# First attention of a four-layer kernel: plain products for the first keys, GpSimd's sums and loads in a written order, two roots on ScalarE, another order of the key and value products

## The chip, the cores and the metric

The kernel runs on one core of one Trainium2 chip. A core has five engines that work at the same time, each through its own instructions in order: TensorE (PE in the profile, with its weight loads as PEld), VectorE (DVE), ScalarE (ACT), GpSimd (POOL) and SyncE (SP), which here only starts transfers. The metric is the device time of one execution in microseconds (us). The time before is the median of three runs.

## The reference

Four layers work one after the other on `x` (2048 rows of 512 features, float32), each adding its result to `x`: cross attention, a feed-forward network, a second cross attention, a mixture of experts. The change is in the first:

```python
def _L0_xattn_ref(query, kv, Wq, bq, Wkv, bkv, Wo, bo):
    q = (query @ Wq + bq).reshape(B, L, NKV, G, HDIM)
    k_, v_ = jnp.split(kv @ Wkv + bkv, 2, axis=-1)
    ...
    scores = jnp.einsum('blkgd,bmkd->bkglm', q, k) * scale
    attn = jax.nn.softmax(scores, axis=-1)
    o = jnp.einsum('bkglm,bmkd->blkgd', attn, v).reshape(B, L, NHEAD * HDIM)
    return o @ Wo + bo

x = x + _L0_xattn_ref(_layernorm(x, axis=-1), ctx_4096, ...)
```

There are 32 sequences of 64 rows, 8 key/value heads (NKV) with 4 query heads each (G), and 128 features to a head.

## The kernel before, in words

The 2048 rows are four chunks of 512. The first attention goes through 32 steps `i`; a step is one chunk and one key/value head, and two chunks alternate: for chunks 0 and 1 the eight heads in turn, then the same for chunks 2 and 3. Step 16 is the first of chunk 2, step 17 the first of chunk 3.

**Products in seven parts.** A product of two matrices of 2 by 2 blocks needs eight block products. The kernel uses a scheme with seven, which needs sums and differences of blocks beforehand: `left_sums` makes three sums of the blocks of the left matrix and overwrites one block with a difference, `right_sums` does the same for the right one. Each is four operations. For the weights and the context they run on POOL, for the normalised rows and the attention output on DVE. The products are named after the blocks: "11", "12", "22" and "21" are blocks as they are, "1" to "4" are the sums.

**Where the operands come from.** `attn0_in(c)` prepares a chunk: statistics of the rows by `row_stats` (DVE, L363 and L364 for each of four tiles of 128 rows), the inverse square root of the variance by `inv_sqrt` (DVE: a first guess from the bits of the number, L346, then three rounds of three Newton operations, L353 to L355), the normalised rows `h_a` (DVE, L461), the addition of the output bias `bo` to `x` (POOL, L464), 16 transposes `pt_a` on PE (L468), four copies by ACT (L473), and the four sums on DVE (L424 to L427). `kv_left` makes the sums of a key or value weight for two heads, `ctx_right` those of a chunk of the context, `open_visit` those of the query weight, all on POOL; the output weight's sums follow (`visits[..]["o"]`).

**Making keys and values.** `attn0_kv` makes the keys (`value` 0) or the values (`value` 1) of two heads for one chunk, with seven products on PE (L520). Keys are 128 by 256 in a product, values two of 128 by 128. The products add up in PSUM banks `x`, `z` and two called `y` (`px`, `pz`, `py`, `pw` in the profile). `keep` copies a state of `x` to SBUF on ACT (`u_k`, `u_v`, L529 and L531), and `close` adds a bank and a kept state on DVE into one half of a head's tile (`kv`, L537). A bank that is added into again must first have been read. Of a key's matmuls of 128 by 256 the profile counts two passes each, so that a product is "x4".

**One step.** PE works through the queries of step `i` (`attn0_queries`: seven products of "x8" into `pqx`, `pqy`, `pqz`, `pqv`, L442; ACT adds the bias, L578; DVE closes into `qT_a`, L585), mixed with the turn of the last step's attention weights (`pt_o`, L639), their product with the values (`po_o`) and the output product (`attn0_out`: `ppx_o`, `ppy_o`, `ppz_o`; DVE adds to `x`, L672). After the queries come the scores (`sc_a`) and their softmax on DVE and ACT (L381 to L388). At the end of step `i`, `attn0_in` prepares the next step's chunk if it is new, and `make_kv` makes one set of keys or values. Before step 0 the kernel prepares chunk 0, the sums of the first key weight, the context of chunk 0, the first value weight, the query weight and the output weight, and makes the first keys.

**What sets the order.** A scheduler orders the instructions of each engine. An instruction that is wrapped in `pin` keeps the place that the program gives it among the other pinned ones of its engine. Before the change all of PE's products in this layer are pinned, but nothing on POOL, and on DVE none of the instructions named here. So the scheduler could take the statistics of chunks 2 and 3 early: they stand on DVE within the first 60 us.

**Loads.** SP starts the transfers in the order of the program: `x` of chunk 0, the first key weight, the context of chunk 0, the first value weight, the first query weight and output weight; `x` and context of chunk 1; `x` of chunks 2 and 3; then the weights of the next visit, and eight transfers of 4 MB that clear a buffer of the last layer (`xg<-zero`). A transfer waits until the eighth one before it has landed.

Of the kernel before, what the change touches and what calls it, by code (L numbers as in the profile page):

```python
# [16 lines left out]
P = 128  # L17
# [12 lines left out]
def layers(ctx: ExitStack, tc: tile.TileContext, a: dict, out: bass.AP):  # L30
# [81 lines left out]
    def rows(ap):  # L112
        return ap.rearrange("(k p) n -> p k n", p=P)

    def part(w, at, k, n):
        return w[:, at : at + k * n].rearrange("p (k n) -> p k n", k=k)

    def load_attn0(g, slot):
        w = weights[:, slot]
        wq, wo = part(w, 0, KT, 512), part(w, 3072, 4, HID)  # L120
        nc.sync.dma_start(wq, rows(a["Wq"][:, g * 512 : (g + 1) * 512]))
        nc.sync.dma_start(wo, rows(a["Wo"][g * 512 : (g + 1) * 512, :]))
        return wq, wo

    def load_kv(g, value):

        w = part(weights[:, value], 2048, KT, 2 * P)
        at = (value * NG + g) * P
        nc.sync.dma_start(w, rows(a["Wkv"][:, at : at + 2 * P]))
        return w  # L130
# [58 lines left out]
    def load_ctx(c, dst):  # L189
        src = rows(a["ctxT"][:, c * CH : (c + 1) * CH])  # L190
        if len(dst.shape) == 4:

            for j in range(2):
                for i in range(2):
                    nc.sync.dma_start(
                        dst[:, 2 * j + i], src[:, 2 * j : 2 * j + 2, i * 256 : (i + 1) * 256]
                    )
        else:
            nc.sync.dma_start(dst, src)

    for c in range(NC):
        for i in range(c * TT, (c + 1) * TT):
            nc.sync.dma_start(xs[i], a["x"][i * P : (i + 1) * P, :])
        if c == 0:
            w_k = load_kv(0, 0)
            load_ctx(0, ctx_q[0])
            w_v = load_kv(0, 1)
            w_next = load_attn0(0, 0)
        if c == 1:
            load_ctx(1, ctx_q[1])  # L210

    def constant(name, shape, src):
        t = const.tile(shape, F32, tag=name, name=name)
# [141 lines left out]
            nc.vector.scalar_tensor_tensor(y, u, 1.5, y, ALU.add, ALU.mult)  # L355
        return y

    def row_stats(tiles, name, rms=False):

        mv = small.tile([P, len(tiles), 2], F32, tag="mv", name=f"mv_{name}")  # L360
        for t, x in enumerate(tiles):
            st = small.tile([P, 6], F32, tag="bnst", name=f"st_{name}_{t}")
            nc.vector.bn_stats(st, x)  # L363
            nc.vector.bn_aggr(mv[:, t, :], st)  # L364
        v = small.tile([P, len(tiles)], F32, tag="var", name=f"v_{name}")
        if rms:


            nc.vector.tensor_scalar(
                v, mv[:, :, 1], 1.0 + EPS, EPS * EPS, ALU.mult, ALU.add  # L370
            )
        else:
            nc.vector.tensor_scalar(v, mv[:, :, 1], EPS, None, ALU.add)
        return mv, inv_sqrt(v, name)

    def softmax(dst, ps, scale, name):

# [9 lines left out]
        nc.vector.reciprocal(rs, sm)  # L387
        nc.vector.tensor_tensor(d3, d3, rs[:, :, None].broadcast_to([P, 8, 64]), ALU.mult)  # L388

    def chunk_stats(c, name, rms=False):  # L390
        return row_stats(xs[c * TT : (c + 1) * TT], name, rms)


    def q_heads(qT, h):
# [16 lines left out]
    def left_sums(engine, a11, a12, a21, a22, sums):  # L411

        s1, s2, s4 = sums if isinstance(sums, list) else (sums[:, i] for i in range(3))
        engine.tensor_tensor(s1, a21, a22, ALU.add)  # L414
        engine.tensor_tensor(s2, s1, a11, ALU.subtract)
        engine.tensor_tensor(a21, a11, a21, ALU.subtract)
        engine.tensor_tensor(s4, a12, s2, ALU.subtract)
        return {"11": a11, "12": a12, "22": a22, "1": s1, "2": s2, "3": a21, "4": s4}
# [31 lines left out]
    def w_quarters(w):  # L450

        return [w[:, 2 * i : 2 * i + 2, j * 256 : (j + 1) * 256] for i in range(2) for j in range(2)]

    def attn0_in(c):

        hx = rows_q[c % 2]
        mv, rstd = chunk_stats(c, f"a{c}")
        for t in range(TT):
            x = xs[c * TT + t]
            h = t2(f"h_a{c}_{t}")  # L460
            nc.vector.tensor_scalar(  # L461
                h, x, mv[:, t, 0:1], rstd[:, t : t + 1], ALU.subtract, ALU.mult
            )
            nc.gpsimd.tensor_tensor(x, x, bo, ALU.add)  # L464
            pt = ps_mm(f"pt_a{c}_{t}")
            for k in range(KT):
                pin(
                    nc.tensor.transpose(  # L468
                        pt[:, k * P : (k + 1) * P], h[:, k * P : (k + 1) * P], ident
                    )  # L470
                )

            nc.scalar.copy(  # L473
                hx[:, t // 2 : t // 2 + 3 : 2, :, (t % 2) * P : (t % 2) * P + P],
                pt.rearrange("p (i k n) -> p i k n", i=2, k=2),
            )
        return right_sums(nc.vector, hx[:, 0], hx[:, 1], hx[:, 2], hx[:, 3], hx[:, 4:7])
# [16 lines left out]
    def kv_left(w, value):  # L494

        k11, k12, k21, k22 = (
            w[:, 2 * j : 2 * j + 2, i * P : (i + 1) * P] for i in range(2) for j in range(2)
        )
        return left_sums(nc.gpsimd, k11, k12, k21, k22, kv_sums[value])

    def ctx_right(c):
        x = ctx_q[c % 2]
        return right_sums(nc.gpsimd, x[:, 0], x[:, 1], x[:, 2], x[:, 3], ctx_sums[c % 2])

    def attn0_kv(value, g, c, left, right):
        n = f"{'kv'[value]}{g}_{c}"
        for i in range(2):
            kv[value, g + i, c] = kv_free.pop(0)
        dst = [kv_tiles[:, kv[value, g + i, c], :] for i in range(2)]

        def product(ps, x, y, first=True):
            x, y = left[x], right[y]
            for m in range(2 if value else 1):
                for k in range(2):
                    sides = (y[:, k, m * P : (m + 1) * P], x[:, k, :]) if value else (
                        x[:, k, :], y[:, k, :]
                    )
                    out_ps = ps[:, m * P : (m + 1) * P] if value else ps[:, 0:256]
                    pin(
                        nc.tensor.matmul(  # L520
                            out_ps, *sides, start=first and m == k == 0, stop=k == 1,
                            skip_group_check=True,
                        )
                    )

        def keep(ps, i, name):
            u = t2(f"{name}_{n}")[:, 0:256]
            if value:
                nc.scalar.copy(u, ps[:, 0:256])  # L529
            else:  # L530
                nc.scalar.activation(  # L531
                    u, ps[:, 0:256], AF.Identity, bias=bkv[:, g + i : g + i + 1]
                )
            return u

        def close(i, half, ps, u):
            nc.vector.tensor_tensor(  # L537
                dst[i][:, half * 256 : half * 256 + 256], ps[:, 0:256], u, ALU.add
            )

        x = ps_tr(f"px_{n}")
        product(x, "11", "11")
        u1 = keep(x, 0, "u1")
        y = ps_mm(f"py_{n}")
        product(y, "12", "21")
        close(0, 0, y, u1)
        product(x, "2", "2", first=False)
        u2 = keep(x, 0, "u2")
        z = ps_mm(f"pz_{n}")
        product(z, "1", "1")  # L550
        product(x, "3", "3", first=False)
        u3 = keep(x, 1, "u3")
        close(1, 1, z, u3)
        y = ps_mm(f"pw_{n}")
        product(y, "22", "4")
        close(1, 0, y, u3)
        product(z, "4", "22", first=False)
        close(0, 1, z, u2)

    def kv_use(value, g, c):  # L560

# [4 lines left out]
    def attn0_queries(g, c, left, right):  # L566
# [15 lines left out]
            return u  # L582

        def close(heads, half, ps, u):
            nc.vector.tensor_tensor(  # L585
                q5[:, heads, :, 4 * half : 4 * half + 4, :],
                ps.rearrange("p (m b q) -> p m b q", m=2, q=64),
                u.rearrange("p (m b q) -> p m b q", m=2, q=64),
                ALU.add,
            )  # L590

        x = ps_tr(f"pqx_{n}")
# [111 lines left out]
    def open_visit(v):  # L704

        w = w_next
        k11, k12, k21, k22 = w_quarters(w[0])
        visits[v] = {"w": w, "q": left_sums(nc.gpsimd, k11, k21, k12, k22, wq_sums)}

    def kv_chunk(p, j):  # L710

# [4 lines left out]
        attn0_kv(value, g, c, kv_lefts[value], ctx_rights[c])  # L716

    rights = {0: attn0_in(0)}
    kv_lefts = [kv_left(w_k, 0), None]
    ctx_rights = {0: ctx_right(0)}  # L720
    kv_lefts[1] = kv_left(w_v, 1)
    open_visit(0)
    visits[0]["o"] = right_sums(nc.gpsimd, *w_quarters(visits[0]["w"][1]), wo_sums)
    make_kv(0, 0, 0)
    last = None
    NP = NC // 2 * NG // 2
    for i in range(len(order) + 1):
# [46 lines left out]
        if i + 1 < len(order):  # L774
            cn, gn = order[i + 1]
            if cn not in rights:
                rights[cn] = attn0_in(cn)

        p, step = divmod(i, 4)
        if i == 0:  # L780
            ctx_rights[1] = ctx_right(1)
            make_kv(0, 0, 1)
        if step < 2:
            make_kv(1, p, step)
# [884 lines left out]
```

## Time and profile before

| | us |
|---|---|
| time, median of 3 runs | 1995.72 (1993.96 to 1996.13) |
| the profiled execution | 1996.16 |
| its span, first to last instruction | 1994.5 |
| PE busy | 1894.7 |
| DVE busy | 1060.4 |
| POOL busy | 545.8 |
| ACT busy | 506.0 |
| mean granted clock of PE | 0.983 |

The span's 40 slices of 50 us each (a digit is the busy share in tenths, in the row PEclk the clock that PE was granted):

```profile
PE   4999999999999999999999999999999999979993
PEclk8999999999999999999999999999999999989997
```

The first attention takes slices 1 to 25, and the first slice stands out. The rest of the span is the three other layers, which the diff does not touch. A line of a timeline gives start, duration, engine, line, operation, what is written and read, and how many; in brackets how long the engine was idle before and who ended it. A line of the waits gives the waiting engine, line and tile, who ended the wait, the sum, the number and the longest.

### The profile page before, as it was taken

The page shows a single profiled execution, that of the slowest core. Times are in us where ns is not written, and L with a number is a line of the kernel's source. Part 1 is how long each engine was busy: PE and PEld are TensorE (multiplying, and loading weights), DVE is VectorE, ACT ScalarE, POOL GpSimd, SP SyncE. Part 2 cuts the span into 40 slices and gives each one's busy share as a digit, 9 for nine tenths or more (in the row PEclk, how much of TensorE's full clock was granted, in tenths as well). Part 3 has the DMA queues.
Part 4 walks back from the last instruction along what each step waited for, and adds up shares of the span by engine and source line. Part 5 has one row for each costly group of instructions (what it writes and reads, how often), then busy time and mean ns, then how long its engine had stood idle before and what let it go on. Part 6 is the DMA issues. An engine that isn't in the chain of part 4 may idle for free.

```text
span 1994.5 us, 26636 instructions
## 1 busy us (share of the span) xinstructions
PE 1894.7 (95%) x10556; PEld 1544.1 (77%) x10556; DVE 1060.4 (53%) x2095; ACT 506.0 (25%) x985; POOL 545.8 (27%) x581
## 2 busy tenths in 40 slices
PE   4999999999999999999999999999999999979993
PEld 3888988988988888888888898687778777645441
DVE  7554454454456654454454456555466466773415
ACT  1222122122112212112112121311221565542221
POOL 8211211211322311211211212141444535540115
PEclk8999999999999999999999999999999999989997
DMA  9696111111211111100110012100004201224628
GB/s 322 191 306 189 43 32 32 43 32 32 64 53 33 43 32 32 43 33 32 43 32 22 22 52 63 50 1 12 1 22 137 64 12 54 70 85 132 216 92 272
DMA packets 129882, 151.72 MB, mean 76 GB/s; under 512 B 4704, under 2 KB 84384, under 8 KB 129760
## 3 DMA queue, kind: packets, MB, share of 16 engines
q1 hardware_dynamic: 118752, 122.70, 19.5%
q0 software_dynamic: 5392, 17.11, 2.6%
q10 hardware_dynamic: 5616, 10.23, 1.4%
q8 instruction: 84, 1.38, 0.3%
q14 instruction: 38, 0.31, 0.0%
HBM read 92.60 MB, written 56.36 MB: 75 GB/s over the span
## 4 chain that ended last, share of the span: by engine, by line
PE 87%; DVE 6%; ACT 2%; DMA 2%; issue 1%; POOL 1%; POOLq 0%; ACTq 0%; DVEq 0%
PE ppx_o L442 11%; PE pqx_a L442 8%; PE py L106 6%; PE sc_a L106 6%; PE pqz_a L442 6%; PE ppz_o L442 6%; PE po_o L106 3%; PE pp L106 3%; PE ppy_o L442 3%; PE pdx_f L442 3%; PE pqv_a L442 3%; PE pqy_a L442 3%; PE px_v L520 2%; PE phx_f L442 2%; PE px_k L520 2%; PE pz_v L520 2%
## 5 line engine op out<-in xcount | busy, mean ns | idle before, releaser
L383 ACT ACTIVATE at_a<-at_a 128x512 f32<-128x512 f32 x64 | 40.3, 631 | 442.5 <-DVE at_a L382 442.5
L106 PE MATMUL py<-arena,xT 128*128 x312 | 140.8, 593 | 0.6 <-DVE y L1404 0.4
L442 PE MATMUL pqz_a<-arena 128*128 128x256 f32 x512 | 122.8, 383 | 8.9 <-DVE qT_a L585 8.9
L442 PE MATMUL ppx_o<-weights,oT_o 128*128 128x256 f32 x512 | 122.8, 383 | 0.1
L578 ACT ACTIVATE u_a<-pqx_a,bq 128x256 f32<-128x256 f32 x192 | 80.6, 471 | 165.6 <-PE pqx_a L442 83.1
L106 PEld LDWEIGHTS sc_a<-kv,qT_a 128*128 128x128 f32 x1024 | 120.4, 193 | 1.8
L442 PE MATMUL pqx_a<-arena,weights 128*128 128x256 f32 x512 | 121.0, 379 | 0.0
L106 PE MATMUL sc_a<-kv,qT_a 128*128 128x64 f32 x1024 | 118.7, 274 | 0.0
L442 PEld LDWEIGHTS pqz_a<-arena 128*128 128x128 f32 x512 | 98.3, 192 | 22.8 <-issue 9.3
L672 DVE TENSOR_TENSOR x<-ppx_o,x 128x512 f32<-128x512 f32 x128 | 86.9, 679 | 43.3 <-PE ppx_o L442 38.5
L442 PEld LDWEIGHTS ppx_o<-weights,oT_o 128*128 128x128 f32 x512 | 94.8, 190 | 12.0 <-ACT oT_o L662 0.5
L585 DVE TENSOR_TENSOR qT_a<-pqz_a,u_a 128x512 f32<-128x512 f32 x64 | 44.2, 691 | 112.4 <-ACT u_a L578 79.2
L442 PEld LDWEIGHTS pqx_a<-arena,weights 128*128 128x128 f32 x512 | 94.9, 190 | 11.6
L106 PEld LDWEIGHTS py<-arena,xT 128*128 128x128 f32 x312 | 56.1, 190 | 56.7 <-issue 56.2
L424 POOL TENSOR_TENSOR arena<-weights 128x512 f32<-128x512 f32 x16 | 20.3, 1271 | 273.0 <-PE ppz_o L442 273.0
L585 DVE TENSOR_TENSOR qT_a<-pqy_a,u_a 128x512 f32<-128x512 f32 x32 | 22.1, 691 | 121.4 <-PE pqy_a L442 121.4
L414 POOL TENSOR_TENSOR arena<-weights 128x512 f32<-128x512 f32 x18 | 22.9, 1273 | 218.0 <-PE pqz_a L442 213.7
L414 POOL TENSOR_TENSOR kv_room<-weights 128x256 f32<-128x256 f32 x16 | 12.1, 758 | 254.8 <-DMA weights<-in_Wkv 254.7
L1404 DVE TENSOR_TENSOR y<-py,weights 128x512 f32<-128x512 f32 x39 | 26.9, 691 | 84.9 <-PE py L106 77.2
L381 DVE TENSOR_REDUCE mx_a<-sc_a 128x8 f32<-128x512 f32 x64 | 44.3, 692 | 45.1 <-PE sc_a L106 45.1
L106 PE MATMUL po_o<-atT_o,kv 64*128 64x256 f32 x512 | 65.9, 392 | 0.8 <-ACT atT_o L641 0.8
L953 POOL TENSOR_TENSOR s_f<-s_f,arena 128x512 f32<-128x512 f32 x16 | 21.4, 1359 | 157.0 <-DVE s_f L950 117.1
(402 smaller groups left out, 4242.8 us busy)
## 6 DMA issues: line engine op xcount, KB each, us to landing
xg<-zero SPq DMA_DIRECT2D x8, 4096.0 KB, 20.7
weights<-in_Wq SPq DMA_DIRECT2D x16, 1024.0 KB, 5.3
weights<-in_Wo SPq DMA_DIRECT2D x16, 1024.0 KB, 5.3
xr<-xg SPq DMA_DIRECT2D x39, 256.0 KB, 3.2
yg<-y ACTq DMA_DIRECT2D x39, 256.0 KB, 2.8
weights<-in_Wkv SPq DMA_DIRECT2D x16, 512.0 KB, 3.5
arena<-in_W_e SPq DMA_DIRECT2D x8, 1024.0 KB, 6.6
x<-in_x SPq DMA_DIRECT2D x16, 256.0 KB, 5.6
```

Source lines behind the costliest of these rows:

```text
L106: nc.tensor.matmul(ps, lhsT, rhs, start=(i == 0), stop=(i == len(pairs) - 1))
L381: nc.vector.tensor_reduce(mx, p3, AX.X, ALU.max)
L383: nc.scalar.activation(dst, dst, AF.Exp, scale=scale)
L414: engine.tensor_tensor(s1, a21, a22, ALU.add)
L424: engine.tensor_tensor(t1, b12, b11, ALU.subtract)
L442: nc.tensor.matmul(ps[:, m, :], left[:, k, m * P : (m + 1) * P], right[:, k, :], start=first and m == i == k == 0, stop=i == len(pairs) - ...
L520: nc.tensor.matmul(out_ps, *sides, start=first and m == k == 0, stop=k == 1, skip_group_check=True,)
L578: nc.scalar.activation(u[:, m * 256 : (m + 1) * 256], ps[:, m * 256 : (m + 1) * 256], AF.Identity, bias=bq[:, 4 * g + 2 * heads + m : 4 * ...
L585: nc.vector.tensor_tensor(q5[:, heads, :, 4 * half : 4 * half + 4, :], ps.rearrange("p (m b q) -> p m b q", m=2, q=64), u.rearrange("p (m ...
L672: nc.vector.tensor_tensor(dst, ps.rearrange("p (m n) -> p m n", m=2), dst, ALU.add)
L953: nc.gpsimd.tensor_tensor(y, y, gamma, ALU.mult)
L1404: pin(nc.vector.tensor_tensor(y, py, be1[:, bass.ds(v[1], 1), :], ALU.add))
```

## The change

- **First keys.** `make_kv(0, 0, 0)` is replaced by `attn0_first_keys`: for each of the two heads one plain product over all 512 features, 128 by 512, and one eviction by ACT with the bias. It needs no sums.
- **POOL's order.** In the start all of POOL's sums and bias adds are pinned, through the class `InOrder`, in this order: query weight, first key weight, context of chunk 1, first value weight, context of chunk 0, bias of chunk 0, output weight, and after step 0's scores the bias of chunk 1. After that POOL is free again. The bias adds leave `attn0_in` and become `add_bias`.
- **Loads.** The first query weight stands before the first value weight, and the latter and the first output weight are moved behind `x` and the context of chunk 1.
- **Roots.** For chunks 0 and 1 `first_inv_sqrt` takes a logarithm and an exponential on ACT and one round of Newton on DVE. Chunks 2 and 3 keep `inv_sqrt`.
- **Statistics.** For chunks 2 and 3 the statistics are pinned, and so is DVE's `close` of the queries, everywhere.
- **Key and value products.** `z`'s first product and its own kept state come right after `x`'s first; `z` gets its second product after `x`'s second, and the last one is `x`'s third. There are four kept states instead of three, in two tiles instead of three. `close` uses other pairs of bank and kept state.

```diff
         if c == 0:
             w_k = load_kv(0, 0)
             load_ctx(0, ctx_q[0])
-            w_v = load_kv(0, 1)
-            w_next = load_attn0(0, 0)
+            w_next = load_queries0(0, 0)
         if c == 1:
             load_ctx(1, ctx_q[1])
+            w_v = load_kv(0, 1)
+            w_next = w_next, load_out0(0, 0)
...
+    def first_inv_sqrt(v, name):
+
+        y = small.tile(v.shape, F32, tag="rsqrt", name=f"rs_{name}")
+        nc.scalar.activation(y, v, AF.Ln)
+        nc.scalar.activation(y, y, AF.Exp, scale=-0.5)
...
+        nc.vector.tensor_tensor(u, y, y, ALU.mult)
+        nc.vector.tensor_tensor(u, u, half, ALU.mult)
+        nc.vector.scalar_tensor_tensor(y, u, 1.5, y, ALU.add, ALU.mult)
+        return y
...
-            nc.vector.bn_stats(st, x)
+            stats = nc.vector.bn_stats(st, x)
+            if pinned:
+                pin(stats)
...
+    class InOrder:
+
+
+        def tensor_tensor(self, *operands):
+            pin(nc.gpsimd.tensor_tensor(*operands))
+
+    adder = [InOrder()]
+
+    def add_bias(c):
+        for x in xs[c * TT : (c + 1) * TT]:
+            adder[0].tensor_tensor(x, x, bo, ALU.add)
...
-        mv, rstd = chunk_stats(c, f"a{c}")
+        roots = first_inv_sqrt, inv_sqrt
+        mv, rstd = chunk_stats(c, f"a{c}", root=roots[c // 2], pinned=c > 1)
...
-            nc.gpsimd.tensor_tensor(x, x, bo, ALU.add)
...
         x = ps_tr(f"px_{n}")
         product(x, "11", "11")
-        u1 = keep(x, 0, "u1")
+        u1 = keep(x, 0, 0)
+        z = ps_mm(f"pz_{n}")
+        product(z, "1", "1")
+        z1 = keep(z, 1, 1)
         y = ps_mm(f"py_{n}")
         product(y, "12", "21")
         close(0, 0, y, u1)
         product(x, "2", "2", first=False)
-        u2 = keep(x, 0, "u2")
-        z = ps_mm(f"pz_{n}")
-        product(z, "1", "1")
-        product(x, "3", "3", first=False)
-        u3 = keep(x, 1, "u3")
-        close(1, 1, z, u3)
+        u2 = keep(x, 0, 2)
+        product(z, "4", "22", first=False)
+        close(0, 1, z, u2)
         y = ps_mm(f"pw_{n}")
         product(y, "22", "4")
+        product(x, "3", "3", first=False)
+        u3 = keep(x, 1, 3)
+        close(1, 1, x, z1)
         close(1, 0, y, u3)
-        product(z, "4", "22", first=False)
-        close(0, 1, z, u2)
+
+    def attn0_first_keys(g, c, w):
+
+        x = ctx_q[c % 2]
+        for i in range(2):
+            kv[0, g + i, c] = kv_free.pop(0)
+            ps = ps_mm(f"pk_{g + i}_{c}")
+            accumulate_next(
+                ps.rearrange("p (i n) -> p i n", i=2),
+                [
+                    (w[:, k, i * P : (i + 1) * P], x[:, k // 2 * 2 : k // 2 * 2 + 2, k % 2, :])
+                    for k in range(KT)
+                ],
+            )
+            nc.scalar.activation(
+                kv_tiles[:, kv[0, g + i, c], :], ps, AF.Identity,
+                bias=bkv[:, g + i : g + i + 1],
+            )
...
-            nc.vector.tensor_tensor(
-                q5[:, heads, :, 4 * half : 4 * half + 4, :],
...
+            pin(
+                nc.vector.tensor_tensor(
+                    q5[:, heads, :, 4 * half : 4 * half + 4, :],
...
     rights = {0: attn0_in(0)}
+    attn0_first_keys(0, 0, w_k)
+    open_visit(0)
     kv_lefts = [kv_left(w_k, 0), None]
-    ctx_rights = {0: ctx_right(0)}
+    ctx_rights = {1: ctx_right(1)}
     kv_lefts[1] = kv_left(w_v, 1)
-    open_visit(0)
-    visits[0]["o"] = right_sums(nc.gpsimd, *w_quarters(visits[0]["w"][1]), wo_sums)
-    make_kv(0, 0, 0)
+    ctx_rights[0] = ctx_right(0)
+    add_bias(0)
+    visits[0]["o"] = right_sums(adder[0], *w_quarters(visits[0]["w"][1]), wo_sums)
...
                 rights[cn] = attn0_in(cn)
+                if cn > 1:
+                    add_bias(cn)
...
         if i == 0:
-            ctx_rights[1] = ctx_right(1)
+            add_bias(1)
+            adder[0] = nc.gpsimd
             make_kv(0, 0, 1)
```

The diff leaves the loads of later visits and the three other layers as they are.

## The prediction

> **What bounds the kernel now.** I read the page, then the waits by engine, then the timeline of the first 110 us, of two steady rounds and of the place where chunks 2 and 3 enter.
>
> ```profile
> PE 1894.7 (95%) x10556; PEld 1544.1 (77%) x10556; DVE 1060.4 (53%) x2095; ACT 506.0 (25%) x985; POOL 545.8 (27%) x581
> ```
>
> TensorE (PE) is the bound. From 100 to 1200 us it is busy more than 99.4 us in every 100, so time can come only from PE's gaps. The waits of PE that lie in the code of the diff:
>
> ```profile
> PE pqz_a L442 <- DVE qT_a L585: 8.9, 1, 8.9
> PE px_k L520 <- POOL kv_room L425: 6.8, 1, 6.8
> PE pz_k L520 <- DVE kv L537: 3.8, 16, 0.6
> ```
>
> The first two are single gaps of the start, the third a small one met in each key product. In the timeline (start, duration):
>
> ```profile
> 11.24 2.89 PE L468 MATMUL pt_a<-ident,h_a 128*128 128x128 f32 x12 [11.24 <-DVE h_a L461]
> 15.84 1.45 DVE L424 TENSOR_TENSOR arena<-arena 128x512 f32<-128x512 f32 x1 [1.39 <-ACT arena L473]
> 17.83 1.71 POOL L424 TENSOR_TENSOR kv_room<-arena 128x512 f32<-128x512 f32 x1
> 23.75 2.08 PE L520 MATMUL px_k<-kv_room 128*128 128x256 f32 x4 [6.84 <-POOL kv_room L425]
> 50.27 3.75 PE L442 MATMUL pqz_a<-arena 128*128 128x256 f32 x8 [8.90 <-DVE qT_a L585]
> ```
>
> The gap before 23.75 waits for GpSimd's (POOL) sums, which stand behind its bias adds. The one before 50.27 waits for VectorE (DVE), which had the statistics of chunks 1, 2 and 3 and their roots in front of `qT_a`. DVE and POOL slow each other: a DVE sum of two SBUF tiles takes about 0.69 us alone and 1.45 here, POOL's 1.27 becomes 1.71. The PE timeline goes on:
>
> ```profile
> 74.37 1.04 PE L639 MATMUL pt_o<-ident,at_a 128*128 128x128 f32 x8
> ...
> 146.02 1.05 PE L520 MATMUL px_k<-arena,weights 128*128 128x256 f32 x4
> 146.91 1.03 PE L520 MATMUL pw_k<-kv_room,weights 128*128 128x256 f32 x4
> 148.16 1.13 PE L520 MATMUL pz_k<-arena,kv_room 128*128 128x256 f32 x4 [0.22 <-DVE kv L537]
> 149.13 1.04 PE L639 MATMUL pt_o<-ident,at_a 128*128 128x128 f32 x8
> ```
>
> 74.37, the first `pt_o`, ends the start. Products of four key matmuls begin 0.86 us apart, the last only after 1.25: it adds into `z`, which DVE must first have read. Where chunk 2 enters:
>
> ```profile
> 628.43 0.68 DVE L388 TENSOR_TENSOR at_a<-at_a,rs_a 128x512 f32<-128x512 f32 x1
> 628.49 1.91 PE L468 MATMUL pt_a<-ident,h_a 128*128 128x128 f32 x16
> 629.03 0.68 DVE L672 TENSOR_TENSOR x<-ppx_o,x 128x512 f32<-128x512 f32 x1
> ```
>
> PE transposes at 628.49 without waiting: `h_a` was made from 607.59 to 618.15, from statistics taken at 44 to 48 us. DVE adds the last product of the round only after that. And what a gap costs beyond itself (stretch, length, PE, PEld, DVE, ACT, POOL, granted clock, DMA, GB/s):
>
> ```profile
> 44.00:48.00 4.00, 0.00 (x0) 0.00 (x0) 3.86 (x14) 0.00 (x0) 0.00 (x0) 0.67 1.15 346
> 48.00:52.00 4.00, 1.73 (x4) 1.49 (x5) 4.00 (x10) 0.00 (x0) 2.73 (x2) 0.50 0.25 75
> 52.00:56.00 4.00, 4.00 (x18) 3.55 (x17) 2.96 (x9) 0.00 (x0) 1.84 (x2) 0.55 0.00 0
> 56.00:60.00 4.00, 4.00 (x39) 4.00 (x38) 2.31 (x5) 1.15 (x3) 0.69 (x1) 1.00 0.00 0
> ```
>
> The clock falls to 0.5 some 4 us into the gap and is back at about 55.6, 5.3 us after work resumed: half of that, 2.7, is lost. After the gap of 6.84 us the same reckoning gives 2.3. I take 2.5.
>
> **The change, part by part.**
>
> *Start.* I follow the new order on each engine. Loads: the first transfers land at 256 KB per 0.69 us in the order issued (`x` 4 to 7 at 22.2 to 24, chunk 1's context at 25.0 to 27.2). So with the second Wkv and Wo moved behind chunk 1, Wq (1 MB, 2.75 us) lands behind the first context (14.6) at 17.4 instead of 18.8, `x` 4 to 7 from 18.0 to 20.1, context 1 from 20.8 to 22.9, Wkv at 24.3, Wo at 27.0. The later SP items keep their places and total.
>
> Root: six of nine Newton steps (0.2 us each) and the bit trick leave DVE, two ScalarE (ACT) operations come. No such small one is in the trace; a 128x256 one from SBUF takes 0.415, a 128x512 one 0.631, so 128x4 is about 0.2 by the line through them (bounds 0 and 0.415). With a hand-over each way the root is 0.7 us shorter (0.2 to 1.1). POOL's bias adds are gone from beside `h_a`, so four of them take 4 x 0.52 rather than 3.83: PE's transposes end at 12.5, ACT's four copies at 14.0, DVE's four sums at 16.6 (POOL idles until Wq).
>
> First keys: two products of K=512, 16 passes of 128x512 at 0.43 us (rows `py` of the experts: eight begin in 3.43) are 6.9 us, against 6.05 for seven shared ones, but need none of POOL's sums. They start when context 0 is there, 13.2, and end at 20.1. Queries: seven products of 1.73 us from 20.1. POOL's Wq sums (17.5 + 4 x 1.27 = 22.6) come in time. ACT now holds `pk_1`'s eviction and the first `u_a` behind the root of chunk 1, which waits for `x` 7 and DVE to 21.5: PE loses 0.2. DVE has three Newton steps, two contended `h_a` (1.42 each) and the closes; the last query product waits for one of them 0.1, the scores 0.9. Scores 32.6 to 37.0, transposes to 38.7 (before: 60.1), keys of chunk 1 38.7 to 45.3.
>
> Now DVE is late: softmax, its multiplication and the four sums of chunk 1, six operations with two SBUF tiles against POOL's row of sums and bias adds, 1.4 to 1.7 each, put the close that frees `py_v`'s bank at 51.0, where PE wants it at 47.0: 4 us. `pt_o` begins at 55.6. **Start: 74.4 - 55.6 = -18.8.** Bounds: -23 without that wait; -13.5 with the half clock after it (2.5) and Wq landing behind `x` 4 to 7 (2.75). POOL's remaining list (context 0, bias 0, Wo sums, bias 1; 16 x 1.27 and what DVE takes) ends near 61; Wo's sums are wanted by the third product of `attn0_out`, near 74. If that cover were gone, PE would wait one for one.
>
> *Order of the key and value products.* `z`'s second product now comes three products after its eviction, and the last closes fall under `pt_o`. A key bank takes 6.56 us now (142.57 to 149.13) against 7 x 0.865 = 6.05, a value bank 6.60 against 6.25. In the steady part are 14 and 15 of them: **-12.4** (7.1 + 5.3). The fourth eviction (0.37 to 0.47 on ACT, 25% busy) and `u3` after the last product lie under `pt_o` and two query products. Bound: 0, if `pt_o` has to wait instead.
>
> *Statistics of chunks 2 and 3.* They are pinned, and so are DVE's closes, so DVE can't take them early: the built order has them behind the round's last add. PE's transposes stand next. Chunk 2: with T the start of the last product, the add begins at T+1.93, the first statistics at T+2.65; three more at 0.79; from the last statistics to `h_a` 3.26 (rows 7.29 to 10.55, the root stays on DVE), to the transposes 0.69 (10.55 to 11.24): T+8.97 instead of T+1.73. Wait 7.2 and clock 2.5: **+9.7**. Chunk 3: seven statistics of the next stage and their small operations stand between; back to back at 0.6 and 0.1 to 0.2, `h_a` starts 9.6 after the first: T+12.94, wait 11.2, clock 2.5: **+13.7**. Upper bound there: eleven at 0.79 and thirty small at 0.21 are 15.0, wait 16.6. Lower: 9. The cover lost is 20 us of DVE's spare time.
>
> Row: after 50.27 real products ran, at half clock for 5.3 us. [...] The sum takes 2.5.
>
> *Bias adds* of chunks 2 and 3 go behind their transposes on POOL (27% busy), under the next 20 us of PE.
>
> **Sum**: -18.8 - 12.4 + 9.7 + 13.7 = **-7.8**. The profiled run took 1996.16 (span 1994.5 and 1.66 around it), 0.44 over the median; from the median, 1995.72 - 7.8 = **1988**.
>
> **Rivals.**
> 1. *The bank waits only move* (slower). Place: the end of each key or value set, `pt_o` waiting for closes. Price 12.4: 1995.7 - 18.8 + 23.4 = 2000; it decides from 7.8 kept, 0.27 per bank. For it: three evictions and three closes still end behind the last product. Against: `pt_o`'s two banks were read products earlier. 0.12.
> 2. *The start gives less*: -13.5, so 1993. For it: ACT and DVE work in order behind chunk 1's root. Against: landings follow the order of issue. 0.18.
> 3. *No wait at `py_v`*: -23, 1984. For it: in the steady part DVE's contended sums took 1.1 to 1.2. 0.15.
> 4. [...] 0.10.
>
> **How the numbers follow.** The forecast has 0.45, its own range 1983 to 1993. A measurement here tells 0.2% (4 us) from no change: faster is under 1991.7, slower over 1999.7. Faster: 0.42 of the forecast, all of rival 3, a third of rival 2: 0.63. Slower: most of rival 1 and some of 4: 0.13. Between: 0.24. Range 1980 to 1998: rivals 2, 3 and 4 are in it, rival 1's upper end is not.
>
> **What would show it.** The first `pt_o` near 55.6, no long PE wait before 38, one of some 4 us at `py_v`; key banks of 6.05 and value banks of 6.25; PE waits of 7 and 11 us at `pt_a` behind `h_a` for chunks 2 and 3, with the clock at 0.5 after each. I am wrong if those two waits are missing (then 1965) or `pt_o` comes after 62.

## The result, and the profile after

The changed kernel takes 1987.36 us (median of nine runs, 1986.13 to 1991.57). The kernel before took 1996.13 us beside it (1993.96 to 2005.25). The ratio is 0.9947 with a 95% interval of 0.9929 to 0.9964, so the kernel is faster by 0.4 to 0.7%: 8.8 us between the medians, some 11 by the ratio. The prediction said 1988 and faster. The profiled execution took 1988.88 us, its span is 1987.0.

Small as it is, this is the sum of two large amounts. Page of the changed kernel, busy time of each engine, and from its waits by engine two lines (sum, number of times, longest):

```profile
PE 1888.4 (95%) x10544; PEld 1545.4 (78%) x10544; DVE 1056.9 (53%) x2077; ACT 519.9 (26%) x1019; POOL 548.3 (28%) x581
```

```profile
PE pt_a L502 <- DVE h_a L496: 28.2, 5, 10.3
...
PE py_v L554 <- DVE kv L573: 3.6, 1, 3.6
```

The waits at `pqz_a`, `px_k` and `pz_k` that the page of before led with are gone. `pt_a` now leads: its 28.2 us hold the 10.3 us up to the first `h_a` of all (11.2 before) and two new waits for chunks 2 and 3. The timeline of TensorE (PE), changed kernel, shows the start and one steady key bank (start, duration):

```profile
10.34 3.65 PE L502 MATMUL pt_a<-ident,h_a 128*128 128x128 f32 x16 [10.34 <-DVE h_a L496]
13.78 7.49 PE L106 MATMUL pk<-arena,weights 128*128 128x512 f32 x16
21.11 1.89 PE L464 MATMUL pqx_a<-arena,weights 128*128 128x256 f32 x8
...
33.45 3.84 PE L106 MATMUL sc_a<-kv,qT_a 128*128 128x64 f32 x32
...
38.88 1.03 PE L554 MATMUL px_k<-arena,weights 128*128 128x256 f32 x4
...
50.45 1.16 PE L554 MATMUL py_v<-weights,arena 128*128 128x128 f32 x8 [3.57 <-DVE kv L573]
...
55.01 1.04 PE L696 MATMUL pt_o<-ident,at_a 128*128 128x128 f32 x8
...
122.87 1.03 PE L554 MATMUL px_k<-arena,weights 128*128 128x256 f32 x4
...
128.91 1.04 PE L696 MATMUL pt_o<-ident,at_a 128*128 128x128 f32 x8
```

The start ends at 55.01 instead of 74.37, the two gaps of 6.84 and 8.90 us in it are gone, and one of 3.57 at `py_v` has come. A key bank takes 128.91 - 122.87 = 6.04 us instead of 6.56. What was paid for it stands where chunk 2 enters. First VectorE (DVE), then PE, changed kernel:

```profile
603.29 0.69 DVE L729 TENSOR_TENSOR x<-ppx_o,x 128x512 f32<-128x512 f32 x1
603.90 0.68 DVE L383 BATCH_NORM_STATS2 st_a<-x 128x6 f32<-128x512 f32 x1
...
609.40 3.82 DVE L496 TENSOR_SCALAR h_a<-x,mv_a,rs_a 128x512 f32<-128x512 f32 x4
```

```profile
601.36 1.89 PE L464 MATMUL ppx_o<-arena,oT_o 128*128 128x256 f32 x8
610.09 2.95 PE L502 MATMUL pt_a<-ident,h_a 128*128 128x128 f32 x12 [6.83 <-DVE h_a L496]
613.37 1.08 PE L502 MATMUL pt_a<-ident,h_a 128*128 128x128 f32 x4 [0.33 <-DVE h_a L496]
614.25 1.62 PE L554 MATMUL px_k<-arena,weights 128*128 128x256 f32 x4
...
662.20 2.95 PE L502 MATMUL pt_a<-ident,h_a 128*128 128x128 f32 x12 [10.35 <-DVE h_a L496]
```

DVE begins the statistics only after the round's last addition to `x`; before, `h_a` was ready long ahead. PE stands for 6.83 us, in chunk 3 for 10.35, and goes on slowly: 16 transposes take 4.16 us (610.09 to 614.25) instead of 1.75. The clock tells why. Stretches of the changed kernel around both waits (stretch, length, PE, PEld, DVE, ACT, POOL, granted clock, DMA, GB/s):

```profile
604.00:608.00 4.00, 0.00 (x0) 0.00 (x0) 3.74 (x13) 0.00 (x0) 0.00 (x0) 1.00 0.00 0
608.00:612.00 4.00, 1.91 (x9) 1.64 (x10) 3.74 (x11) 0.59 (x1) 1.98 (x2) 0.58 0.00 0
612.00:616.00 4.00, 3.67 (x15) 3.01 (x15) 2.11 (x2) 1.80 (x4) 3.57 (x3) 0.57 0.00 0
616.00:620.00 4.00, 4.00 (x20) 3.53 (x19) 2.77 (x6) 1.38 (x3) 0.00 (x0) 1.00 0.00 0
...
654.00:658.00 4.00, 0.00 (x0) 0.00 (x0) 3.96 (x15) 0.00 (x0) 0.00 (x0) 0.80 0.16 61
658.00:662.00 4.00, 0.00 (x0) 0.00 (x0) 4.00 (x26) 0.00 (x0) 0.00 (x0) 0.50 0.00 0
662.00:666.00 4.00, 3.47 (x15) 2.83 (x16) 4.00 (x5) 1.76 (x3) 3.87 (x3) 0.50 0.00 0
666.00:670.00 4.00, 4.00 (x35) 4.00 (x34) 3.73 (x20) 1.33 (x3) 1.69 (x2) 0.92 0.00 0
```

The clock record of the trace has only the values 1 and 0.5, so a stretch was at half clock for 2 x (1 - granted clock) of its length. For chunk 2 that gives 3.36 us in 608 to 612 and 3.44 in 612 to 616, so half clock ends near 615.4, 5.3 us after PE resumed; for chunk 3 it ends near 666.6, 4.4 after. Half of these, 2.7 and 2.2 us, is lost on top of the waits.

### The profile page after: what moved, and what is told of

It reads as the page before. It is cut to its first block, busy times and chain, and to the rows that moved or that the text cites. A ratio compares the mean times of both kernels' runs of the same rounds, so it can differ in the third digit from the quotient of the medians.

```text
span 1987.0 us, 26632 instructions
## 1 busy us (share of the span) xinstructions
PE 1888.4 (95%) x10544; PEld 1545.4 (78%) x10544; DVE 1056.9 (53%) x2077; ACT 519.9 (26%) x1019; POOL 548.3 (28%) x581
## 4 chain that ended last, share of the span: by engine, by line
PE 88%; DVE 6%; DMA 2%; ACT 2%; issue 1%; POOL 1%; POOLq 0%; SPq 0%; DVEq 0%; ACTq 0%
PE ppx_o L464 11%; PE pqx_a L464 9%; PE sc_a L106 6%; PE pqz_a L464 6%; PE ppz_o L464 6%; PE py L106 6%; PE po_o L106 3%; PE pp L106 3%; PE pdx_f L464 3%; PE pqv_a L464 3%; PE ppy_o L464 3%; PE pqy_a L464 3%; PE px_v L554 2%; PE phx_f L464 2%; PE px_k L554 2%; PE pq_b L106 2%
```

## The experiments

Three readings of the trace make the runs comparable even where the other layers scatter by a few us: the first `pt_o` (the start), the distance from the first to the last `pt_o` (the steady part), and the ratio to the kernel before on the same chip (medians of 1996 to 2005 us there). A start is read from one profile of each kernel. e1 and e5, whose edits lie behind the start, have their first `pt_o` at 53.3 and 55.6 against 55.0, so differences of up to some 2 us in that column say little by themselves.

| run | first `pt_o` | first to last `pt_o` | ratio | 95% interval |
|---|---|---|---|---|
| before | 74.4 | 1150.2 | 1 | |
| the change | 55.0 | 1160.9 | 0.9947 | 0.9929 to 0.9964 |
| e1, statistics in mid-step | 53.3 | 1137.5 | 0.9832 | 0.9806 to 0.9858 |
| e2, statistics in the start | 61.2 | 1137.5 | 0.9859 | 0.9838 to 0.9880 |
| e3, old key and value order | 60.6 | 1173.5 | 1.0039 | 1.0026 to 1.0052 |
| e4, before + new order alone | 70.8 | 1137.5 | 0.9925 | 0.9902 to 0.9948 |
| e5, no bias in chunks 2 and 3 | 55.6 | 1159.8 | 0.9927 | 0.9909 to 0.9945 |
| e6, roots on DVE | 56.9 | 1161.1 | 0.9946 | 0.9928 to 0.9963 |
| e7, old loads | 56.3 | 1159.6 | 0.9957 | 0.9942 to 0.9972 |
| e8, POOL unpinned | 56.6 | 1161.1 | 0.9943 | 0.9925 to 0.9962 |
| e9, chunk 1's sums on POOL | 51.7 | 1160.9 | 0.9923 | 0.9904 to 0.9942 |
| e11, first keys in seven parts | 57.2 | 1160.9 | 0.9957 | 0.9940 to 0.9974 |
| e12, bias adds first | 57.2 | 1159.6 | 0.9947 | 0.9928 to 0.9967 |
| e10, e1 and e9 together | 52.4 | 1137.5 | 0.9807 | 0.9783 to 0.9831 |

The steady part takes 1137.5 us whenever the new product order stands and PE has no wait at `pt_a` there (e1, e2, e4, e10). With the new order and those waits it takes 1159.6 to 1161.1.

**e1: the statistics of chunks 2 and 3 earlier.**

```diff
+    early = {}
...
-        mv, rstd = chunk_stats(c, f"a{c}", root=roots[c // 2], pinned=c > 1)
+        if c > 1:
+            mv, rstd = early.pop(c)
+        else:
+            mv, rstd = chunk_stats(c, f"a{c}", root=roots[0])
...
+        if i in (11, 13):
+            cn = 2 + (i - 11) // 2
+            early[cn] = chunk_stats(cn, f"a{cn}", root=inv_sqrt, pinned=True)
```

> The changed kernel with one thing moved: the statistics and the root of chunks 2 and 3 are issued at the end of steps 11 and 13, a step and a half before their transposes, still in written order. My theory: the whole loss of the change sits in PE's two waits at pt_a (6.8 and 10.4 us) and the slow work right behind them; the trace has +10.0 and +13.1 us there. Without them 1987.4 - 23 = about 1964 (1960 to 1969), the two waits at pt_a are gone from the list of waits, the granted clock stays at 1.00 there, and the first pt_o stays near 55.0. Rival A, the waits only move (the closes or the softmax stand behind the early statistics, and PE waits for those): 1975 to 1987. Rival B, the 23 us are mostly not the waits but POOL's bias adds beside h_a: those stay, so under 10 us are gained.

The ratio falls from 0.9947 to 0.9832, and the steady part from 1160.9 to 1137.5: 23.4 us. The timeline of e1, DVE and then PE:

```profile
580.53 1.95 DVE L501 TENSOR_SCALAR h_a<-x,mv_a,rs_a 128x512 f32<-128x512 f32 x2
```

```profile
599.70 1.89 PE L464 MATMUL ppx_o<-arena,oT_o 128*128 128x256 f32 x8
601.42 1.91 PE L507 MATMUL pt_a<-ident,h_a 128*128 128x128 f32 x16
603.17 1.03 PE L559 MATMUL px_k<-arena,weights 128*128 128x256 f32 x4
```

With its statistics done, `h_a` starts 20 us before PE needs it, between DVE's other work; PE runs through and the transposes take 1.75 us. My theory holds. Rival A would have shown a new wait, rival B less than 10 us.

**e2: the statistics back in the start.** In `attn0_in`, `pinned=c > 1` becomes `pinned=False`.

> The changed kernel with the pins of the statistics of chunks 2 and 3 taken off: the order that is built puts them into the start again, between the first query closes, as in the kernel before. My theory: the two waits at pt_a go (-23) and the start is longer, since eight statistics (0.6 to 0.8 us each), two roots of 2 us and small operations, some 9 to 12 us of DVE, stand in front of operations that PE waits for at 38 to 50 us: the first pt_o at 59 to 66, 4 to 11 later than 55.0, so 1968 to 1975. Rival: DVE has room for them behind PE's query products, the start stays at 55 and the time is about 1964, as if the statistics cost nothing anywhere.

The steady part is that of e1, and the start 6.2 us longer than the change's (predicted 4 to 11). From the timeline of e2, PE:

```profile
32.85 1.97 PE L464 MATMUL pqz_a<-arena 128*128 128x256 f32 x8 [1.09 <-DVE qT_a L641]
...
36.43 3.56 PE L106 MATMUL sc_a<-kv,qT_a 128*128 128x64 f32 x24 [0.78 <-DVE qT_a L641]
...
55.01 1.64 PE L554 MATMUL py_v<-weights,arena 128*128 128x128 f32 x8 [4.43 <-DVE kv L573]
```

The eight statistics stand in DVE's queue, and PE waits at the query closes and longer at `py_v`. Those waits are 2.7 us more than the changed kernel's; the other 3.4 are half clock, which the trace has from 38.46 to 41.88 and from 55.53 to 58.94 (the transposes at 39.79 take 2.77 us, in the changed kernel 1.75), and the changed kernel has none there. So the statistics in the start cost 6.2 us, half of it by the clock, and where they were put costs 23.4. Mid-step costs neither.

**e3 and e4: the order of the key and value products.** e3 puts the old order into the changed kernel, e4 the new order into the kernel before. The core of the edit in e4 (e3 is its reverse):

```diff
-        u1 = keep(x, 0, "u1")
+        u1 = keep(x, 0, 0)
+        z = ps_mm(f"pz_{n}")
+        product(z, "1", "1")
+        z1 = keep(z, 1, 1)
...
+        product(z, "4", "22", first=False)
+        close(0, 1, z, u2)
...
-        product(z, "4", "22", first=False)
-        close(0, 1, z, u2)
```

> The changed kernel with the old order of the key and value products alone put back. My theory: the order is worth 0.51 us in each of 14 key banks and 0.35 in each of 15 value banks, 12.4 in all, so about 1999.8 (1997 to 2002); a key bank takes 6.56 again and PE's small waits at pz_k are back. Rival, the gain of the banks was given back elsewhere (pt_o or later products waiting): the time stays within 4 us of 1987.

> The kernel before with the new order of the key and value products alone. My theory: the gain adds up on its own, 1996 - 12.4 (and a further 0.4 for the first two banks) = about 1983 (1981 to 1986), which is faster than the whole change. Rival, the order pays only together with the new start: within 4 us of 1996.

The steady part moves by 12.6 us in e3 and by 12.7 in e4, as in both expectations. But both expectations leave something out. In e3 the first `pt_o` comes 5.6 us later, 2.7 of it by half clock from 50.44 to 55.84, so the whole is 18 and not 12.4; the time, 0.9% above the changed kernel, is outside the range I gave. In e4 it comes 3.6 earlier. The timeline of e3, PE:

```profile
44.22 1.03 PE L554 MATMUL pw_k<-kv_room,weights 128*128 128x256 f32 x4
50.44 2.08 PE L554 MATMUL pz_k<-arena,kv_room 128*128 128x256 f32 x4 [5.19 <-DVE kv L571]
```

Where DVE is late, the old order makes PE wait inside the key bank, as `z`'s second product needs a close; the new order lets PE go on until `py_v`, some three products further. The order and the start are not separate terms. e4 reaches the last `pt_o` 7.6 us before the whole change (1208.3 against 1215.9); by the ratio the two are not told apart.

**e5: what makes the restart slow.** The two lines `if cn > 1: add_bias(cn)` are left out.

> The changed kernel without POOL's eight bias adds on chunks 2 and 3 (left out, so these chunks lack the bias bo). It tells apart what makes the 16 transposes after each of the two waits take 4.2 us instead of 1.75. Theory clock: PE is at half clock after its wait, whatever DVE does; h_a takes 1.9 us for four instead of 3.8, but the transposes still take about 3.5, as at the start of the kernel; the two waits themselves stay at 6.8 and 10.4; at most 0.8 us less in each place, 1 to 2 in all. Rival, the transposes are paced by h_a, which POOL's bias adds slow: without them 16 transposes take about 2 us, 2.2 less in each place, some 4.5 in all.

The timeline of e5, DVE and then PE:

```profile
609.98 1.92 DVE L496 TENSOR_SCALAR h_a<-x,mv_a,rs_a 128x512 f32<-128x512 f32 x4
```

```profile
610.67 3.65 PE L502 MATMUL pt_a<-ident,h_a 128*128 128x128 f32 x16 [6.83 <-DVE h_a L496]
614.11 1.89 PE L554 MATMUL px_k<-arena,weights 128*128 128x256 f32 x4
```

`h_a` takes half as long, the transposes still 3.44 us, at a granted clock of 0.63 from 608 to 612 and 0.52 from 612 to 616. So the clock sets their pace and the bias adds cost 0.7 us per chunk, less some 0.25 that `px_k` gives back. The steady part is 1.1 shorter, within the 1.5 us by which it scatters among e6 to e9, e11 and e12.

**e6, e7, e8: three edits of the start undone one by one.** e6: `roots = inv_sqrt, inv_sqrt`. e7: the loads of the first value, query and output weight in front of chunk 1's `x`. e8: `adder = [nc.gpsimd]`.

> The changed kernel with the root of chunks 0 and 1 on DVE again (bit trick and nine Newton steps). My theory: the first transposes come 0.7 us later (11.0 instead of 10.34), and chunk 1's longer root makes DVE 1 to 2 us later in front of the close that frees py_v's bank: the first pt_o at 55.7 to 57.5, so +0.7 to +2.5 on the changed kernel. Rival, the root costs nothing because Wk or the context land later than the transposes end: pt_o stays at 55.0.

> The changed kernel with the old order of the loads (second Wkv, Wq and Wo in front of chunk 1's x). My theory: Wq lands 1.4 us later and POOL's first sum starts at 18.3, still in time for the third query product; x 4 to 7 land 4 us later, and DVE, which works in written order, is later by some 3 to 4 us with chunk 1's statistics, h_a and the query closes: the scores wait 2 to 3 us and the first pt_o comes at 57 to 60, +2 to +5 on the changed kernel. Rival, DVE has slack for it: pt_o within 1 us of 55.0.

> The changed kernel with POOL's sums and bias adds in the scheduler's order instead of the written one. My theory: POOL, idle until 16.9 now, begins with the sums of the keys and of context 0 (8 operations, some 8 us), the sums of Wq end near 27 instead of 22.2, and PE waits for them 2 to 3 us in front of the third query product, at half clock behind it: the first pt_o at 57 to 60, +2 to +5. Rival, the earlier start of POOL empties its queue sooner, DVE's contended sums at 42 to 50 us are faster and the wait at py_v (3.6) shrinks: -1 to -3.

The first `pt_o` comes 1.9, 1.3 and 1.6 us later: inside the expectation for e6, below it for e7 and e8. The ratios don't tell any of the three from the changed kernel. Each trace has a new wait in front: 0.84 us (e6) and 1.24 (e7) for DVE at the last query product, 1.39 (e8) for POOL at the third. At chunk 1's first key product they stand at 39.5, 39.3 and 39.6 against 38.9 (e9, which changes nothing before that point, at 39.4). At `py_v` the difference is gone: it begins at 50.66, 50.08 and 50.41 against 50.45, since DVE's queue decides when PE may go on there, and the waits are shorter (2.8 to 3.2 against 3.57). What is left is a stretch of half clock behind `py_v`, worth some 1.7 us, which all three have and the changed kernel's profile happens not to have (see the end). So none of the three, undone alone, is worth more than the scatter of the start.

**e9: the wait at `py_v`.**

```diff
-        return right_sums(nc.vector, hx[:, 0], hx[:, 1], hx[:, 2], hx[:, 3], hx[:, 4:7])
+        engine = adder[0] if c == 1 else nc.vector
+        return right_sums(engine, hx[:, 0], hx[:, 1], hx[:, 2], hx[:, 3], hx[:, 4:7])
...
```

(The rest of the edit puts the bias adds of chunk 0 and the sums of the output weight behind them.)

> The changed kernel with chunk 1's four sums of the query input moved from DVE to POOL, in front of the bias adds of chunk 0. My theory: the wait of 3.6 us at py_v is DVE's queue (softmax, its multiplication, these four sums at 1.2 to 1.8 each) in front of the key closes; without the sums the closes come before 46 and the wait is gone: the first pt_o near 51.5, the whole 3 to 4 us faster than the changed kernel. Rival, the wait moves to another close or to the next queries, because POOL is 5 us later with the sums of Wo and the bias adds: within 1.5 us of the changed kernel.

The timeline of e9, PE:

```profile
46.31 1.06 PE L555 MATMUL pz_v<-kv_room 128*128 128x128 f32 x8
47.20 1.06 PE L555 MATMUL py_v<-weights,arena 128*128 128x128 f32 x8
```

The wait is gone, the first `pt_o` is 3.3 us earlier although this run's first transposes are 0.3 later, and the ratio falls by 0.0024, or 4.8 us (the intervals overlap). The wait was DVE's queue.

**e11 and e12: what took the 6.84 us gap out.** e11 makes the first keys in seven parts again, e12 moves `add_bias(0)` to the head of POOL's list.

```diff
-    attn0_first_keys(0, 0, w_k)
-    open_visit(0)
     kv_lefts = [kv_left(w_k, 0), None]
-    ctx_rights = {1: ctx_right(1)}
+    ctx_rights = {0: ctx_right(0)}
+    make_kv(0, 0, 0)
+    open_visit(0)
+    ctx_rights[1] = ctx_right(1)
     kv_lefts[1] = kv_left(w_v, 1)
-    ctx_rights[0] = ctx_right(0)
```

> The changed kernel with the first key bank as seven shared products again, POOL's sums for it (keys, then context 0) in front of the sums of Wq, and the bias adds still behind them. It tells whether the plain products themselves took the old wait of 6.8 us out, or the bias adds leaving POOL's head did. My theory, the bias adds did: POOL starts on the keys near 9.6, finishes the 8 sums near 18 to 19, the seven products (6.05 against 7.3) wait 0 to 1.5 us in all, the sums of Wq end near 24, in time for the third query product: the first pt_o at 54 to 57, -1 to +2 on the changed kernel. Rival, the plain products did: PE waits 4 to 7 us before or behind the key products and the first pt_o comes at 59 to 62.

> The changed kernel with the bias adds of chunk 0 put back at the head of POOL's list, where POOL otherwise idles until Wq lands at 16.9. My theory: four h_a beside them take 3.8 us instead of 1.9, but the transposes, at half clock there, end only 0.7 to 1 later; POOL's row at 38.6 to 44.5 is empty of bias adds, so POOL is 5.9 us further when DVE does softmax and the sums of chunk 1, and the wait at py_v shrinks by 1 to 3: the first pt_o at 53 to 55.5, -2 to +0.5 on the changed kernel. Rival, the bias adds at the head are what made the old start slow: with them there the transposes end 2 us later, Wq's sums start a few us later and PE waits for them: pt_o at 57 or later.

The timeline of e11, PE:

```profile
15.01 1.13 PE L554 MATMUL pz_k<-kv_room 128*128 128x256 f32 x4 [0.24 <-POOL kv_room L480]
...
20.05 1.13 PE L554 MATMUL pw_k<-kv_room,weights 128*128 128x256 f32 x4 [1.32 <-POOL kv_room L480]
...
25.94 1.97 PE L464 MATMUL pqx_a<-arena 128*128 128x256 f32 x8 [0.44 <-POOL arena L480]
```

Without the bias adds in front, POOL's sums begin at 10.38, not at 16.70 as in the kernel before, and PE waits 2.0 us for them in all, not 6.84. The plain products are worth 1.6 us at chunk 1's first key product (40.48 against 38.88), and 0.6, which is within the scatter, at `py_v` (51.02 against 50.45); the rest of the later `pt_o` is half clock. e12 shows the other half: bias adds first, plain keys kept, and that product comes only 0.7 later. So either edit takes out most of the gap; the kernel with both undone and all else kept was not tried. In e12 the wait at `py_v` did not shrink (3.42), against my theory: POOL was busy throughout 39 to 51.7 with the next item of its list, and beside it DVE's multiplication and sums took 1.16 to 1.76 us each, where the changed kernel's first sums, with POOL idle, took 0.69 (at 14.64). Its later `pt_o` is 0.5 us from the front (`py_v` at 50.97) and 1.6 of half clock.

**e10: both repairs.**

> Both repairs together: the statistics and the root of chunks 2 and 3 issued at the end of steps 11 and 13, and chunk 1's four sums on POOL in front of the bias adds. My theory: PE's waits at pt_a of chunks 2 and 3 (23 us with their clock) and the one at py_v (3.6) are separate, so the gains add: 26.6 below the changed kernel, about 1961, a ratio of 0.981 to 0.982 to the kernel before (0.9947 for the changed kernel alone); the first pt_o at 51 to 52, none of the three waits in the list. Rival, POOL's longer list at 50 to 70 us or DVE's early statistics take something back: 0.983 or more, no better than the early statistics alone (0.9832).

1961.77 us against 1997.28 beside it, ratio 0.9807. Page of e10:

```profile
PE 1882.4 (96%) x10544; PEld 1541.6 (79%) x10544; DVE 1052.0 (54%) x2073; ACT 518.8 (26%) x1019; POOL 550.4 (28%) x585
```

Start 52.4, steady part 1137.5, and none of the three waits. Its last `pt_o` stands at 1189.9, 26.0 us before the changed kernel's (26.6 expected). Against e1 it gains only 0.9 there, since e1's start had come out 1.7 earlier by itself; by the ratio e10 lies 0.0025 below e1, which their intervals don't separate. So that the gains add is likely, but the rival, no better than e1, is not excluded. e10 beats both kernels, by 1.9% and by 1.4%.

## Why the prediction was right, step by step

- **Start, -18.8 predicted:** -19.4 (74.37 to 55.01). On the way two errors cancelled. The transposes were to end at 12.5 and the keys to start at 13.2; the keys started at 13.78, since 16 transposes took 3.44 us at the pace of half clock, not the pace of `h_a` (1.92, predicted 2.1). The keys took 7.33 instead of 6.9, since full clock came only at 14.69. The scores came at 33.45 (predicted 32.6), but they and the transposes took 5.4 us instead of 6.1, so chunk 1's keys came at 38.88 (38.7). The wait at `py_v` was 3.57 instead of 4, with no half clock behind it. That was luck: of the nine profiles that wait there, seven have a stretch of half clock behind the wait, worth 1.5 to 1.7 us. With it the start would have been some -17.7.
- **What the start is made of** was less clear than the sum made it look. I gave a price to each edit, but undone alone, the loads, POOL's order and the roots are not told from scatter. The runs give 6.2 to the statistics that left (e2, 3.4 of it half clock), 5.6 to the product order (e3, 2.7 of it half clock), 0.6 to the plain keys (e11, without its half clock). Those are effects of removal, they need not add to 19.4, and the two larger ones are about half clock. The 5.6 is the part I missed: I counted the product order in the steady part alone.
- **Root:** two ACT operations of 0.20 us each, as estimated; `h_a` began at 9.65, 0.9 before the old 10.55 (0.7 predicted).
- **Product order, -12.4:** key bank 6.04 (6.05 predicted), value bank 92.07 - 85.82 = 6.25 (6.25); e3 and e4 give 12.6 and 12.7 for the steady part. `pt_o` did not have to wait: rival 1 is refuted.
- **Chunk 2, +9.7:** the wait was 6.83 (7.2), the clock 2.7 (2.5), another 0.33 for the last `h_a`. **Chunk 3, +13.7:** wait 10.35 (11.2), clock 2.2 (2.5). Together, with 0.33 for the last `h_a` of chunk 3, 22.7 by these rows and 23.4 by e1 and e2, against 23.4. In chunk 2 the first statistics began 0.11 us sooner after the last product than I had it, and `h_a` 3.10 us after the last statistics instead of 3.26.
- **The row after 50.27,** one of the two behind the 2.5, has real products behind the wait; here transposes (128x128, f32) stood there. In chunk 2 full clock was back 5.3 us after PE resumed, as in that row. In chunk 3 PE did nothing but transposes from 662.20 to 666.36, with one gap of 0.33 us, and full clock was back at 666.64, 4.4 us after.
- **Rival 2** (start gives less) and **rival 4** (dearer waits at chunks 2 and 3) did not come. No run shows the price that rival 4's chance, 0.10, stands on; half clock cost 2.7 and 2.2 us there. **Rival 3** (no wait at `py_v`, -23 in the start) is the kernel e9: 74.4 - 51.7 = 22.7.
- **Bias adds of chunks 2 and 3 "under PE's next 20 us":** nearly. They double `h_a` to 3.82 us, which costs the 0.7 of e5.

The sum of -7.8 met the time (8.8 between the medians) because its two big sides, some 32 us gained and 23 lost, were each right to within 1 us. At the first `lg_f`, behind this attention, the traces differ by 1257.2 - 1248.5 = 8.7; the spans differ by 7.5, the rest scattered in layers that the diff does not touch.

## What to carry to other kernels

Pinning an instruction takes away the scheduler's freedom to put it into idle time: before pinning work that feeds a bound engine, find the latest point at which it is needed and write it ahead of that, where its engine has room (a step and a half was enough here; less was not tried). The reordering was worth more where an engine was late (e3: 5.6 us in the start) than in the steady state (12.6 over 29 banks), so a reordering's price must be asked in both places. When a change gains little, split it: the new product order alone gave 0.9925, the whole change 0.9947 (not told apart by their intervals), and the whole change without its one bad move 0.9832.

## What the runs showed of the hardware

In the clock records of the kernel before and of the changed one, half clock came in stretches of 3.41, 6.83 and 10.24 us, but for the last stretch, which runs on past the last instruction. The changed kernel has it from 608.61 to 615.44, 6.83 us, and from 656.40 to 666.64, 10.24 us; the old gap that the prediction shows has it from 45.39 to 55.63, 10.24 us.

The length of a wait does not tell by itself whether half clock follows it. The stretches from the wait at `py_v` on, first of the changed kernel, then of e12:

```profile
48.00:52.00 4.00, 1.55 (x14) 1.56 (x14) 3.67 (x7) 0.00 (x0) 4.00 (x3) 1.00 0.97 291
52.00:54.00 2.00, 2.00 (x20) 2.00 (x19) 0.56 (x2) 0.37 (x1) 2.00 (x3) 1.00 1.11 333
54.00:56.00 2.00, 2.00 (x20) 2.00 (x19) 0.38 (x2) 0.72 (x2) 2.00 (x2) 1.00 1.12 331
...
48.00:52.00 4.00, 1.03 (x9) 1.03 (x10) 3.90 (x6) 0.00 (x0) 3.71 (x3) 1.00 1.06 313
52.00:54.00 2.00, 2.00 (x14) 2.00 (x13) 0.42 (x1) 0.37 (x1) 1.50 (x3) 0.58 1.11 332
54.00:56.00 2.00, 2.00 (x12) 2.00 (x12) 0.42 (x1) 0.00 (x0) 1.33 (x2) 0.57 1.06 309
```

The changed kernel's wait of 3.57 us brought nothing, that of e12, 3.42 us, brought half clock. A wait of 2.55 us (e11) brought it, one of 2.47 (e1) did not. What decides is not shown here. The changed kernel, e1 and e5 have the same start; e5's wait of 2.7 us brought half clock that cost 1.5 us, and those of the other two none, so the same start may come out some 1.5 us better or worse.

The clock record of the changed kernel begins only at 14.69 us, and the views show 1.00 for what lies before. There the 16 transposes ran at half pace, in 3.44 us, as they did at half clock in e5 (3.44; at full clock, at 37.13, they took 1.75). Before the record begins, only the durations tell.

A small operation of DVE took 0.17 us with POOL idle and 1.19 beside a sum of POOL's. Two lines of the changed kernel, the same line of code on 128x4 numbers:

```profile
8.58 0.17 DVE L371 TENSOR_SCALAR hf_a<-v_a 128x4 f32<-128x4 f32 x1
...
21.02 1.19 DVE L371 TENSOR_SCALAR hf_a<-v_a 128x4 f32<-128x4 f32 x1
```

At 21.02 a sum of POOL's that takes 1.27 us had begun at 20.92, and the small operation lasted until it ended. Not every operation of DVE was held up: statistics beside POOL's sums at 18.88 took 0.68 us, and 0.66 at 4.53 with no sum of POOL's beside them.
